# Sorting token-expert pairs by expert in a two-layer adaLN kernel: 46 gathered rows in place of all experts on all tokens

## The chip, the core and the metric

The kernel runs on one core of a Trainium2 chip. The core has five engines that work at the same time: TensorE (PE, matrix products into PSUM; PEld is its weight load), VectorE (DVE), ScalarE (ACT), GpSimd (POOL) and SyncE (SP, which issues DMAs). [...] DMAs issued on SP, ACT and POOL all run on the core's 16 DMA engines. The metric is the device time of one execution in microseconds (us), the median of several.

## What is computed

Two blocks of an adaLN network on x of 2 batches x 1024 tokens x 128 features, float32. The first block is a recurrence and six layers of windowed attention with a gated feed-forward part. The second is full attention (16 heads of 64, a bias by distance) and a mixture of experts. The change is in the last part only:

```python
E, F, TOP_K = 8, 512, 2
router_logits = xf @ gate_w                             # [2048, 8]
top_vals, top_idx = jax.lax.top_k(router_logits, TOP_K)
top_w = jax.nn.softmax(top_vals, axis=-1)
cw = jnp.einsum('tk,tke->te', top_w, one_hot(top_idx, E))   # 2 of 8 weights are not zero
for e in range(E):
    h = gelu(xf @ w1[e] + b1[e])                        # 128 -> 512
    out = out + cw[:, e:e + 1] * (h @ w2[e] + b2[e])    # 512 -> 128
```

Here xf is the layer-normed, scaled and shifted stream; the result is gated and added to the stream. Only two experts of each token have a weight other than zero.

## The kernel before

Tokens are worked on in four segments of 512 (two of each batch); features of a segment stand as [128 features, 512 tokens] or, turned, as four tiles of [128 tokens, 128 features]. All products are float32; each is two instructions on TensorE.

The first block (`first_block`, 0 to about 1635 us) writes out the order of PE, DVE, ACT and POOL by hand. The second (`second_block`) writes out PE, DVE and ACT; POOL and SP are placed by the tile scheduler. `attention` goes over 128 tiles of (batch, pair of heads, 128 query tokens), one every 5.86 us: turned probabilities of the tile two back, scores of this one, their maximum (DVE, line 1390), the exponential (ACT, line 1400), the scaling by the sum (POOL, line 1404), the output of the tile three back (line 1426). Once the last head of a segment is through, `attention_projected` (line 1436) makes the new stream and `expert_tokens` appends small pieces of work to a list: norm (`norm_pieces`: tokens, moments, centred, scaled), routing (`routing_pieces`: logits, exponentials, chosen, weights), expert biases (`bias_pieces`). `next_piece` runs one of them per tile, later one per expert. In `centred`, POOL makes `ln_less` (lines 1464, 1465) between two steps of ACT. Batch 0's pieces run in the attention of batch 1; part of batch 1's run in the expert stage.

The expert stage (`experts`) goes over 4 segments x 8 experts. `expert_hidden` makes the 512 hidden features of 512 tokens (line 1617: four products of 128x128 by 512; GELU on ACT, line 1620), `expert_outputs` the four tiles of output (line 1633: 16 products of 128x128 by 128) and adds each, times its token's weight for this expert, to `macc` (DVE, line 1637). `expert_sum` gates, adds the stream and writes the segment out. All weights of the eight experts stay in SBUF; two experts are loaded before the attention, six when it has ended (lines 1510, 1513). PSUM has four double banks throughout the second block.

Of the kernel before, what the change touches and what calls it, by code (L numbers as in the profile page):

```python
# [26 lines left out]
SEG = 512  # L28
# [24 lines left out]


# [37 lines left out]
class Net:  # L92
    def __init__(self, ctx, tc, io):
        self.ctx, self.tc, self.nc, self.io = ctx, tc, tc.nc, io
        nc = self.nc
        self.const = ctx.enter_context(tc.tile_pool(name="const", bufs=1))
        self.stream = ctx.enter_context(tc.tile_pool(name="stream", bufs=1))
        self.stat = ctx.enter_context(tc.tile_pool(name="stat", bufs=3))
        self.n = 0

        self.fixed = self.const.tile([128, NCONST], F32, tag="fixed", name="fixed")
        nc.scalar.dma_start(out=self.fixed[:, :K_TAB], in_=io["shape_consts"][:, :K_TAB])
        self.cols = self.const.tile([128, NCOLS], F32, tag="cols", name="cols")
        nc.scalar.dma_start(out=self.cols, in_=io["cols"])
        self.ident = self.fixed[:, K_ID : K_ID + 128]
        self.eps = self.const.tile([128, 1], F32, tag="eps", name="eps")
        nc.gpsimd.memset(self.eps, EPS)
# [95 lines left out]
    def recurrence_loads(self):  # L203
# [18 lines left out]
        nc.sync.dma_start(out=self.fixed[:, K_TAB:], in_=io["shape_consts"][:, K_TAB:])  # L222
# [693 lines left out]
    def rotary(self, st, a):  # L916
# [3 lines left out]
        if st.seg < PER_B:  # L920
# [4 lines left out]
            for kind in range(2):  # L925
                j = 2 * a + kind
                tab = self.fixed[:, K_TAB + j * NTT * DH : K_TAB + (j + 1) * NTT * DH]
                tab = tab.rearrange("p (t d) -> p t d", d=DH)[:, t0 : t0 + TT]
                for lo, width, other in ((0, DH, 0),) if kind == 0 else ((0, half, half), (half, half, 0)):
                    nc.gpsimd.tensor_tensor(  # L930
                        rot[:, kind, :, lo : lo + width],
                        tab[:, :, lo : lo + width],
                        sc[:, other : other + width].unsqueeze(1).to_broadcast([128, TT, width]),
                        ALU.mult,
                    )
# [276 lines left out]
    def second_block_opened(self):  # L1212
# [18 lines left out]
        for e in range(2):  # L1231
            self.load_expert(e)
# [10 lines left out]
    def second_block(self):  # L1243
# [4 lines left out]
        engines = {mybir.EngineType.PE, mybir.EngineType.DVE, mybir.EngineType.Activation}  # L1248
        with ExitStack() as es:
            self.psum(es, "two", 0, 4)  # L1250
            with ExitStack() as at:
                work = at.enter_context(tc.tile_pool(name="att_left", bufs=2, side="left"))
                with tc.manual_schedule(engines=engines):
                    self.attention(work)
            self.right.close()
            rest = es.enter_context(tc.tile_pool(name="moe_rest", bufs=2, side="left"))
            for e in range(2, E):
                self.load_expert(e, rest)
            with tc.manual_schedule(engines=engines):
                self.experts(rest)  # L1260
# [5 lines left out]
    def attention(self, work):  # L1266
# [10 lines left out]
        for n in range(len(tiles) + 3):  # L1277
# [19 lines left out]
            self.next_piece()  # L1297
            if last and lc == NP - 1 and lt % TT == TT - 1:
                seg = lb * PER_B + lt // TT
                self.attention_projected(seg, oT[lb])  # L1300
                self.expert_tokens(seg)
            if n < len(tiles) and t in (3, 5) and n + NKT - t < len(tiles):
# [140 lines left out]
    def norm_pieces(self, src, out, scale, bias, b, keep=None):  # L1443
# [15 lines left out]
        def centred():  # L1459
# [7 lines left out]
            for i in range(TT):  # L1467
# [6 lines left out]
                )  # L1474

# [31 lines left out]
    def load_expert(self, e, pool=None):  # L1507
        nc, io = self.nc, self.io
        w1 = self.get(pool or self.mw, [128, F1], f"ew1_{e}", bufs=1)
        nc.sync.dma_start(out=w1, in_=io["ew1"][e])  # L1510
        w2 = self.get(pool or self.mw, [128, F1 // 128, D], f"ew2_{e}", bufs=1)
        queue = nc.gpsimd if pool else nc.sync
        queue.dma_start(out=w2, in_=io["ew2"][e].rearrange("(c p) d -> p c d", p=128))
        self.ew[e] = w1, w2

    def expert_tokens(self, seg):

        b = seg // PER_B
        tokens = self.get(self.moe, [128, TT, D], "x_tok", bufs=NSEG)
        h = self.get(self.moe, [128, SEG], "mh", bufs=NSEG)  # L1520
        self.norm_pieces(self.x3, h, 4, 3, b, keep=tokens)
        cw = self.routing_pieces(h)
        acc = self.get(self.moe, [128, TT, D], "macc", bufs=NSEG)
        self.bias_pieces(cw, acc)
        self.routed[seg] = tokens, h, cw, acc

    def routing_pieces(self, h):
# [4 lines left out]
        cw = self.get(work, [128, TT, E], "cw", bufs=NSEG)  # L1532
        sel = self.get(work, [128, TT, E], "sel")
# [41 lines left out]
        return cw  # L1575
# [20 lines left out]
    def experts(self, work):  # L1596

        order = [(s, e) for s in range(NSEG) for e in range(E)]
        hidden = {}
        for n in range(len(order) + 1):  # L1600
            if n < len(order):
                hidden[n] = self.expert_hidden(work, *order[n])
            if n:
                self.expert_outputs(*order[n - 1], hidden.pop(n - 1))
            self.next_piece()
            if n and order[n - 1][1] == E - 1:
                self.expert_sum(work, order[n - 1][0])

    def expert_hidden(self, work, s, e):
        nc = self.nc  # L1610
        h, w1 = self.routed[s][1], self.ew[e][0]
        hid = self.get(work, [128, F1 // 128, SEG], "hid")
        for i in range(F1 // 256):
            ps = self.two_banks()
            for k in range(2):
                j = 2 * i + k
                nc.tensor.matmul(ps[:, k], w1[:, j * 128 : (j + 1) * 128], h, start=True, stop=True)  # L1617
            for k in range(2):
                j = 2 * i + k
                nc.scalar.activation(  # L1620
                    hid[:, j], ps[:, k], AF.Gelu, bias=self.col(C_EB1 + e * 4 + j)
                )
        return hid

    def expert_outputs(self, s, e, hid):
        nc = self.nc
        _, _, cw, acc = self.routed[s]
        w2 = self.ew[e][1]
        ps = self.bank()
        for t in range(TT):  # L1630
            tok = slice(t * 128, (t + 1) * 128)
            for j in range(F1 // 128):
                nc.tensor.matmul(  # L1633
                    ps[:, tok], hid[:, j, tok], w2[:, j], start=(j == 0), stop=(j == F1 // 128 - 1)
                )
        for t in range(TT):
            nc.vector.scalar_tensor_tensor(
                acc[:, t],
                ps[:, t * 128 : (t + 1) * 128],
                cw[:, t, e : e + 1],  # L1640
                acc[:, t],
                ALU.mult,
                ALU.add,
            )

    def expert_sum(self, work, s):
        nc = self.nc
        tokens, _, _, acc = self.routed[s]
        gate = self.gates[:, s // PER_B].unsqueeze(1).to_broadcast([128, TT, D])
        o = self.get(work, [128, TT, D], "o")  # L1650
        nc.vector.tensor_tensor(o, acc, gate, ALU.mult)
        nc.vector.tensor_tensor(o, o, tokens, ALU.add)
        nc.sync.dma_start(
            out=self.io["out"][s * SEG : (s + 1) * SEG].rearrange("(i p) d -> p i d", p=128), in_=o
        )
# [104 lines left out]
```

## Time and profile before

| | us |
|---|---|
| median of 3 runs (2808.8 to 2812.72) | 2810.84 |
| the profiled execution | 2810.53 |
| its span in the profile | 2808.8 |
| attention and all before it, to the last projection's end | 2572.4 |
| expert stage, to the end | 236.4 |
| busy in the span: PE / DVE / ACT / POOL | 2674.5 / 1917.5 / 1760.1 / 1582.8 |
| mean granted TensorE clock | 0.994 |
| all DMA: 37.62 MB, mean | 13 GB/s |

Times in the profile are counted from the span's start. A row of the timeline has the start, the duration, the engine, the source line, the operation, tiles as out<-in, the count, and in brackets the idle time before it with what ended that. The time of a page's line is busy time of that engine; engines overlap, so busy times do not add up to the span. "L1633" is line 1633 of the kernel before; the changed kernel has other line numbers.

### The profile page before, as it was taken

The numbers are of one execution on the slowest core, as the hardware profiler recorded it, in microseconds if no ns is written. First come the engines' busy times: TensorE is split into PE (matmuls) and PEld (weight loads), VectorE is DVE, ScalarE is ACT, GpSimd is POOL, SyncE is SP. The second block draws the span as 40 slices with busy tenths as digits, with TensorE's granted clock in tenths as the row PEclk, the third lists the DMA queues.
The fourth block names the chain that finished last, engine by engine and source line by source line (L and its number), as shares of the span: only waits on it lengthen the run. The fifth ranks groups of instructions, "written<-read, shape, count | busy, mean of one in ns | idle before, by whom it ended". The sixth has DMA issues, their size and how long they took to land.

```text
span 2808.8 us, 67320 instructions
## 1 busy us (share of the span) xinstructions
PE 2674.5 (95%) x29476; PEld 1784.6 (64%) x29476; DVE 1917.5 (68%) x2664; ACT 1760.1 (63%) x2514; POOL 1582.8 (56%) x1223
## 2 busy tenths in 40 slices
PE   7899999999999999999999989999999999999999
PEld 4466666666666666666666646666666666666776
DVE  6788788787878787888788746666566666663211
ACT  6467777777777677777777755555544555554533
POOL 4687888788787878788788613333333333331000
PEclk9999999999999999999999999999999999999999
DMA  3000100000010001000000010000000000001000
GB/s 132 1 2 2 32 2 9 32 2 2 9 32 2 6 4 32 2 9 2 2 2 2 17 53 7 10 10 7 7 11 7 7 7 7 1 1 46 4 5 8
DMA packets 24208, 37.62 MB, mean 13 GB/s; under 512 B 1862, under 2 KB 19404, under 8 KB 22892
## 3 DMA queue, kind: packets, MB, share of 16 engines
q1 hardware_dynamic: 22780, 30.29, 3.5%
q8 instruction: 232, 3.80, 0.6%
q0 software_dynamic: 704, 2.43, 0.3%
q10 hardware_dynamic: 432, 0.61, 0.1%
q14 instruction: 60, 0.49, 0.1%
HBM read 32.24 MB, written 1.08 MB: 12 GB/s over the span
## 4 chain that ended last, share of the span: by engine, by line
PE 68%; ACT 15%; DVE 12%; issue 3%; POOL 2%; DMA 0%; ACTq 0%; POOLq 0%; DVEq 0%
PE two L1374 8%; PE proj L948 8%; PE two L1413 7%; PE two L1426 6%; PE two L1123 5%; PE two L1104 5%; ACT px L1113 4%; PE two L1633 4%; PE two L1617 4%; PE two L1019 4%; DVE turned L974 2%; PE two L1039 2%; DVE qk L967 2%; PE two L1190 2%; PE two L1204 2%
## 5 line engine op out<-in xcount | busy, mean ns | idle before, releaser
L1404 POOL TENSOR_SCALAR ap<-ap,a_den 128x1024 f32<-128x1024 f32 x256 | 283.9, 1121 | 578.3 <-DVE a_den L1403 578.2
L985 POOL TENSOR_TENSOR qk<-qk,turned 128x1024 f32<-128x1024 f32 x192 | 453.8, 2363 | 192.1 <-DVE turned L974 185.2
L1400 ACT ACTIVATE ap<-two,a_neg 128x1024 f32<-128x1024 f32 x256 | 285.1, 1114 | 294.2 <-DVE a_neg L1390 287.8
L1390 DVE TENSOR_REDUCE a_neg<-two 128x1 f32<-128x1024 f32 x256 | 301.1, 1217 | 170.7 <-PE two L1374 170.7
L1123 PEld LDWEIGHTS two<-px,wvo 128*128 128x128 f32 x3072 | 356.7, 192 | 57.2 <-issue 29.9
L948 PE MATMUL proj<-wqk,xs 128*128 128x512 f32 x764 | 370.6, 608 | 22.6 <-DVE turned L974 21.1
L1123 PE MATMUL two<-px,wvo 128*128 128x128 f32 x3072 | 362.0, 276 | 17.3 <-ACT xw L1085 17.1
L997 POOL TENSOR_TENSOR qk<-qk,w_inv 128x1024 f32<-128x1024 f32 x192 | 361.7, 1906 | 3.9 <-ACT w_inv L994 2.9
L1413 PEld LDWEIGHTS two<-fixed,ap 128*128 128x128 f32 x2048 | 223.4, 141 | 138.6 <-issue 122.0
L1413 PE MATMUL two<-fixed,ap 128*128 128x128 f32 x2048 | 277.6, 279 | 15.0 <-ACT ap L1400 12.6
L959 ACT ACTIVATE sq<-proj 128x1024 f32<-128x1024 f32 x191 | 195.9, 1026 | 134.3 <-PE proj L948 133.5
L967 DVE TENSOR_TENSOR qk<-proj,rot 128x1024 f32<-128x1024 f32 x191 | 232.5, 1217 | 49.4 <-ACT sq L959 43.9
L1374 PE MATMUL two<-ak,aq 64*128 64x512 f32 x1024 | 259.3, 618 | 2.9 <-DVE gates L1505 1.6
L1426 PE MATMUL two<-apT,av 128*64 128x128 f32 x4096 | 254.2, 277 | 4.3 <-ACT apT L1416 4.3
L1113 ACT COPY px<-two 128x1024 f32<-128x1024 f32 x192 | 195.1, 1017 | 76.5 <-PE two L1104 76.5
L1426 PEld LDWEIGHTS two<-apT,av 128*64 128x64 f32 x4096 | 223.2, 138 | 25.4 <-issue 20.5
L1071 POOL TENSOR_TENSOR p<-p,w_den 128x1024 f32<-128x1024 f32 x96 | 183.3, 1909 | 98.1 <-DVE ya L1133 86.3
L1019 PEld LDWEIGHTS two<-fixed,qk 128*128 128x128 f32 x1536 | 165.1, 141 | 110.9 <-issue 80.9
L974 DVE TENSOR_TENSOR turned<-proj,rot 128x1024 f32<-128x1024 f32 x191 | 231.8, 1213 | 1.5 <-POOL qk L985 1.5
L948 PEld LDWEIGHTS proj<-wqk,xs 128*128 128x128 f32 x764 | 133.1, 191 | 147.2 <-issue 110.9
L1019 PE MATMUL two<-fixed,qk 128*128 128x128 f32 x1536 | 204.1, 277 | 20.7 <-ACT px L1113 13.0
L982 DVE TENSOR_REDUCE w_ss<-sq 128x16 f32<-128x1024 f32 x192 | 221.2, 1191 | 1.5 <-ACT sq L959 1.5
(271 smaller groups left out, 4310.9 us busy)
## 6 DMA issues: line engine op xcount, KB each, us to landing
wqk<-in_wqkv SPq DMA_DIRECT2D x6, 1024.0 KB, 11.5
abias<-rel_turned SPq DMA_DIRECT2D x32, 192.0 KB, 3.0
wv<-in_wqkv SPq DMA_DIRECT2D x6, 512.0 KB, 3.6
wo<-in_wo SPq DMA_DIRECT2D x6, 512.0 KB, 4.1
ew<-in_ew SPq DMA_DIRECT2D x10, 256.0 KB, 4.1
w<-in_w SPq DMA_DIRECT2D x6, 341.0 KB, 8.4
aqkv<-in_aqkv SPq DMA_DIRECT2D x1, 1536.0 KB, 6.7
ew<-in_ew POOLq DMA_DIRECT2D x6, 256.0 KB, 6.8
```

Of the source, the lines that this page charges most:

```text
L948: self.nc.tensor.matmul(ps[:, g], x.step.xs[:, c0 : c0 + 128], x.step.weights[:, a, g * 512 : (g + 1) * 512], start=True, stop=True,)
L967: nc.vector.tensor_tensor(dst, ps.rearrange("p a (h d) -> p (a h) d", d=DH), cos.unsqueeze(1).to_broadcast([128, H, DH]), ALU.mult,)
L974: nc.vector.tensor_tensor(x.turned, halves[:, :, ::-1], sin.rearrange("p (e d) -> p e d", e=2).unsqueeze(1).to_broadcast([128, H, 2, half] ...
L985: self.nc.gpsimd.tensor_tensor(x.qk[a], x.qk[a], x.turned.rearrange("p h e d -> p h (e d)"), ALU.add)
L997: engine.tensor_tensor(x.qk[a], x.qk[a], x.inv[:, a].unsqueeze(2).to_broadcast([128, H, DH]), ALU.mult)
L1019: nc.tensor.transpose(ps[:, c // 4, c % 4 * 128 : (c % 4 + 1) * 128], flat[:, c * 128 : (c + 1) * 128], self.ident,)
L1113: self.nc.scalar.copy(x.px[:, 2 * i : 2 * i + 2].rearrange("p b h q -> p b (h q)"), x.mixed[i])
L1123: nc.tensor.matmul(x.out[:, 0, :128].rearrange("p (b q) -> p b q", q=BLK), merged[:, c // 4, par, c % 4], x.px[:, :, h], start=(h == 0), s ...
L1374: nc.tensor.matmul(scores[par][:, j], q[r, tok], k[r, j * 512 : (j + 1) * 512], start=True, stop=True)
L1390: self.nc.vector.tensor_reduce(neg, ps, AX.XY, ALU.max, negate=True)
L1413: self.nc.tensor.transpose(ps[:, j // 4, j % 4 * 128 : (j % 4 + 1) * 128], p[:, j * 128 : (j + 1) * 128], self.ident)
L1426: nc.tensor.matmul(ops[r, :128], v[:, j, r], pT[par][:, j], start=(j == 0), stop=(j == NKT - 1))
```

## The change

A batch has 1024 tokens and so 2048 pairs of token and chosen expert. The pairs are sorted by expert into rows of 128 slots, each expert beginning a new row: 23 rows (`ROWS = 2 * NKT + E - 1`) hold any choice; what isn't filled is padding. A row has one expert.

Once both segments of a batch are routed, five new pieces (`dispatch_pieces`) make the plan: `counted` (TensorE: how many pairs of an expert stand before each token, and the totals), `placed` (DVE: each pair's slot and each row's expert), `spread` (DVE: one-hot tiles of slot places and token numbers), `listed` (TensorE: their products are the token number of each slot) and `shared` (DVE: the two weights of each token). `centred` also writes the centred tokens to memory. Each row then is gathered from there by an indirect DMA on POOL, turned by TensorE, scaled and shifted, sent through its expert, and written to memory; each token's two outputs are gathered back from there and summed. The weights of a row's expert are loaded for each row anew, from a table in memory (4112 B for each of 128 partitions) that is built beforehand; SP reads the expert's number into a register first. PSUM is eight single banks in the expert stage. In this stage the order of POOL and SP is written out by hand, too.

In `experts`, step n turns row n, makes the hidden features of row n - 1 and the outputs of row n - 3, and runs two pieces. Batch 1's 23 gathers are issued when its plan is there; the condition `(1, 0) not in gathered` holds again in the step after row (1, 0) was taken, and the 23 are issued a second time. POOL's order is: 10 gathers of batch 0 in the attention (with the weights of two rows on SP); 13 at the start of the stage; the last segment's `ln_less`; 23 and 23 of batch 1; 16 of token outputs of batch 0; 16 of batch 1. The token sums of batch 0 begin at step 29, one tile every two steps.

```diff
         with ExitStack() as es:
-            self.psum(es, "two", 0, 4)
+            self.disp = es.enter_context(tc.tile_pool(name="dispatch", bufs=1, side="left"))
+            self.dispatch_tables()
             with ExitStack() as at:
+                self.psum(at, "two", 0, 4)
                 with tc.manual_schedule(engines=engines):
                     self.attention(work)
             self.right.close()
-            for e in range(2, E):
-                self.load_expert(e, rest)
-            with tc.manual_schedule(engines=engines):
+            self.psum(es, "moe", 8, 0)
+            with tc.manual_schedule(engines=engines | {ET.Pool, ET.SP}):
                 self.experts(rest)
...
             self.next_piece()
+            if n >= len(tiles):
+                self.next_piece()
...
                 self.expert_tokens(seg)
+                if seg % PER_B == PER_B - 1:
+                    self.dispatch_pieces(lb)
...
+            if home is not None:
+                nc.sync.dma_start(out=home, in_=xc)
...
+    def dispatch_tables(self):
+        self.table = home("expert_rows", [E, 128, EW])
+        nc.sync.dma_start(out=self.table[:, :, :F1], in_=io["ew1"])
+        for e in range(E):
+            nc.sync.dma_start(
+                out=self.table[e, :, F1 : 2 * F1].rearrange("p (c d) -> p c d", d=D),
+                in_=io["ew2"][e].rearrange("(c p) d -> p c d", p=128),
+            )
...
+    def dispatch_pieces(self, b):
+        def counted():
+            nc.tensor.matmul(ps[:, : NKT * E], self.earlier, flat, start=True, stop=False)
...
+        def spread():
+            for c in range(2):
+                hot = self.onehot().rearrange("p (t f) -> p t f", f=128)
+                nc.vector.tensor_tensor(
+                    hot,
+                    place[:, c * NKT : (c + 1) * NKT].unsqueeze(2).to_broadcast([128, NKT, 128]),
+                    self.count.unsqueeze(1).to_broadcast([128, NKT, 128]),
+                    ALU.is_equal,
+                )
...
+        def listed():
+            for i, (c, t) in enumerate(pairs):
+                nc.tensor.matmul(ps[:, :ROWS], st["hot"][c][:, t], st["ids"][:, c, t], start=i == 0, stop=i == len(pairs) - 1)
...
+        self.pieces += [counted, placed, spread, listed, shared]
...
     def experts(self, work):
-        order = [(s, e) for s in range(NSEG) for e in range(E)]
+        order = [(b, j) for b in range(B) for j in range(ROWS)]
+        for j in range(len(gathered), ROWS):
+            gathered[0, j] = self.slots_gathered(work, 0, j)
+        for n in range(len(order) + 4):
             if n < len(order):
-                hidden[n] = self.expert_hidden(work, *order[n])
+                while loads < len(order) and loads < n + 12 and order[loads][0] in self.plan:
+                    weights[loads] = self.row_weights(work, *order[loads])
+                    loads += 1
+            if n < len(order):
+                if order[n][0] == 1 and (1, 0) not in gathered:
+                    for j in range(ROWS):
+                        gathered[1, j] = self.slots_gathered(work, 1, j)
+                feats[n] = self.row_features(work, order[n][0], gathered.pop(order[n]))
+            if 0 <= n - 1 < len(order):
+                hidden[n - 1] = self.row_hidden(work, feats.pop(n - 1), weights[n - 1])
+            if 0 <= n - 3 < len(order):
+                self.row_outputs(work, *order[n - 3], hidden.pop(n - 3), weights.pop(n - 3))
+            for _ in range(2):
+                self.next_piece()
+            k = n - ROWS
+            if n >= ROWS + 6 and (k - 6) % 2 == 0 and (k - 6) // 2 < NKT:
+                self.token_sums(work, 0, (k - 6) // 2)
+            if 1 in self.plan and (1, 0) not in gathered and n < ROWS - 1:
+                for j in range(ROWS):
+                    gathered[1, j] = self.slots_gathered(work, 1, j)
+        for t in range(NKT):
+            self.token_sums(work, 1, t)
...
+    def slots_gathered(self, work, b, j, bufs=ROWS):
+        x = self.get(work, [128, D], "slots", bufs=bufs)
+        self.nc.gpsimd.indirect_dma_start(
+            x, None, self.centred_rows[b], bass.IndirectOffsetOnAxis(self.plan[b][1][:, j : j + 1], axis=0)
+        )
+    def row_weights(self, work, b, j, bufs=12):
+        e = nc.values_load(self.plan[b][0][0:1, j : j + 1], engines={mybir.EngineType.SP}, min_val=0, max_val=E - 1)
+        w = self.get(work, [128, EW], "row_w", bufs=bufs)
+        nc.sync.dma_start(out=w, in_=self.table[bass.ds(e, 1)].rearrange("o p c -> (o p) c"))
+    def row_features(self, work, b, x):
+        nc.tensor.transpose(ps[:, :128], x, self.ident)
+        nc.vector.tensor_scalar(
+            h, ps[:, :128], self.mod1[:, 4, b : b + 1], self.mod1[:, 3, b : b + 1], ALU.mult, ALU.add
+        )
+    def row_hidden(self, work, h, w):
...
+    def row_outputs(self, work, b, j, hid, w):
...
+        y = self.get(work, [128, D], "row_y", bufs=4)
+        nc.vector.tensor_copy(y, ps[:, :D])
+        nc.sync.dma_start(out=self.output_rows[b][j * 128 : (j + 1) * 128], in_=y)
+    def token_sums(self, work, b, t):
+        for c in range(2):
+            y = self.get(work, [128, D], "pair_y", bufs=2 * NKT)
+            nc.gpsimd.indirect_dma_start(
+                y, None, self.output_rows[b], bass.IndirectOffsetOnAxis(slots[:, c, t : t + 1], axis=0)
+            )
+            nc.vector.scalar_tensor_tensor(
+                acc[:, i], y, share[:, c, t : t + 1], acc[:, i], ALU.mult, ALU.add
+            )
+        nc.vector.tensor_tensor(o, acc[:, i], self.gates[:, b], ALU.mult)
+        nc.vector.tensor_tensor(o, o, tokens[:, i], ALU.add)
+        nc.sync.dma_start(out=self.io["out"][seg * SEG + i * 128 : seg * SEG + (i + 1) * 128], in_=o)
```

## The prediction

> **What bounds the kernel now.** I read the page's busy shares first, then the chain of waits from the end of the attention on, then the stretch tables for the DMA rate, then the timeline for the price of one POOL transfer and for the slack of the engines around it.
>
> The page (engine totals; the shares of the chain):
>
> ```profile
> PE 2674.5 (95%) x29476; PEld 1784.6 (64%) x29476; DVE 1917.5 (68%) x2664; ACT 1760.1 (63%) x2514; POOL 1582.8 (56%) x1223
> ...
> PE 68%; ACT 15%; DVE 12%; issue 3%; POOL 2%; DMA 0%; ACTq 0%; POOLq 0%; DVEq 0%
> ```
>
> TensorE is the bound, and DMA is nowhere. The chain of waits in the expert stage (start, duration, engine, tile, line, instructions):
>
> ```profile
> 2583.89 3.44 PE two L1617 x8
> 2587.33 3.57 PE two L1633 x32
> 2590.90 3.44 PE two L1617 x8
> ```
>
> One expert on one segment of 512 tokens is 7.01 us of TensorE with nothing between, and there are 32 of them. The stretch table (busy us of PE, PEld, DVE, ACT, POOL; granted clock; DMA share; GB/s):
>
> ```profile
> 2572.40:2808.80 236.40, 230.46 (x1329) 168.39 (x1327) 50.16 (x171) 95.87 (x149) 4.97 (x8) 1.00 0.06 19
> ...
> 2575.00:2577.00 2.00, 2.00 (x12) 1.44 (x11) 0.18 (x1) 1.55 (x4) 2.00 (x4) 1.00 1.03 363
> 2577.00:2579.00 2.00, 2.00 (x6) 0.89 (x5) 0.01 (x1) 0.65 (x2) 0.44 (x1) 1.00 1.03 341
> 2579.00:2581.00 2.00, 2.00 (x12) 1.28 (x11) 0.00 (x0) 1.55 (x4) 0.00 (x0) 1.00 1.05 331
> ```
>
> The stage to be replaced lasts 236.4 us at full clock; with all DMA engines busy (share 1) the core reads 331 to 363 GB/s. The timeline, first the price of a POOL transfer, then the slack of POOL in the attention, then the end:
>
> ```profile
> 1.30 1.30 POOL L171 DMA_DIRECT2D sq<-in_wmod  x2 [0.46 <-issue]
> ...
> 2500.93 2.21 POOL L1404 TENSOR_SCALAR ap<-ap,a_den 128x1024 f32<-128x1024 f32 x2 [4.20 <-DVE a_den L1403]
> ...
> 2505.85 1.09 PE L1413 MATMUL two<-fixed,ap 128*128 128x128 f32 x8
> 2506.68 2.21 POOL L1404 TENSOR_SCALAR ap<-ap,a_den 128x1024 f32<-128x1024 f32 x2 [3.54 <-DVE a_den L1403]
> ...
> 2572.86 4.58 POOL L1513 DMA_DIRECT2D ew<-in_ew  x6 [10.17 <-PE two L1436]
> ...
> 2805.50 0.37 SPq L1653 DMA_DIRECT2D out<-o  x1
> ```
>
> POOL issues a plain transfer of 128 rows in 0.65 us (1.30 for two) and one of 512 pieces in 0.76. In the attention it has 3.65 us free in each 5.86 us tile, and a scaled tile (first half done at 2502.0) is wanted 3.8 us later.
>
> **What TensorE saves.** A row of 128 slots is one transpose (0.11 us) and 8 products of 128x128, two instructions each: 16 x 0.112 (3.57 / 32) = 1.8; together 1.9 us. 46 rows are 87 us, against 32 x 7.01 = 224 us. The 896 slots of padding in 2944 are in that. The saving of 137 us is the most there is; the rest says what takes the place of TensorE.
>
> **The unknown price: one gather on POOL, g.** The trace has no indirect transfer. Below, the nearest row is the plain transfer of 128 rows, 0.65 us; above, the longest single POOL instruction of the running kernel, 2.36 us (line 985, two inputs of 128x1024). A gather also has 128 indices to read and 128 addresses to make, so I take twice the plain row, 1.3 us: nearer to the lower end, which is the same kind of instruction. POOL's order in the changed kernel has 101 gathers: 10 in the attention, 13 at the start of the stage, 23 for batch 1, the same 23 again (the condition in `experts` is true a second time once row (1,0) is taken), 16 pairs for batch 0, 16 for batch 1.
> [...]
>
> **The attention of batch 1, where batch 0 is sorted.** TensorE is full there, so its new work is paid: counting and listing are 16 products each, 64 instructions of 0.12 us (0.95 for 8 at line 1538), 7.6 us. DVE has 1.6 us free per tile (5.86 less 2.35, 1.21, 0.45, 0.27). Placing is 13 small operations, 2.8 us (0.18 for 32 elements a row, 0.41 for 256); spreading is 5.0 (two of 128x1024 at 1.21, the others 0.2 to 0.55). Over by 1.2 and 3.4; the rings of scores and turned tiles hide between all and none of that, I take 2.5 lost. The 10 gathers stand on POOL ahead of the next scaling: 13 less 3.65 free less 3.8 slack, 5.6 us for TensorE. Sum **+15.7**. At nothing: building the table in memory (10 copies on SP in layer 0, around layer 1's last two loads, which go out at 31 us and are due over 200 us later; uncovered, 4.2 MB in and out at 345 GB/s would be an estimated 25 us); the writes of centred rows (256 KB, landing 2.3 us by the out rows; batch 0's have 25 tiles before they are read, batch 1's last stands behind twelve weight loads, 12 x 1.5 = 18 us, and is read after t = 47; if late, the same microseconds on every later step); the rotary tables, which only move to another pool; the dropped expert loads, which were hidden. On SP the two first rows' register and weight loads (1 MB, 3.1 us) stand ahead of bias loads that have a lead of some five tiles, 29 us.
>
> **The stage, from 2572.4 on (t = 0: the last projection ends).**
> 1. POOL's 13 gathers wait for the attention's buffers, and the last segment's `ln_less` (lines 1464, 1465 before) is now queued behind them. ScalarE stands at it in order, with it the GELUs of the rows, and TensorE at the next transpose. 13 x 1.3 + 0.5 (ln_less) + 1.65 (centring) + 0.2 + 0.66 + 0.78 + 1.1 (transposes, features, logits) = **21.8**. Some three rows run meanwhile.
> 2. Five steps with two pieces each: exponentials with two table loads of 1.28 and four GELUs of 0.41, 4.4; weights, 2.3; biases and counting on TensorE, 1.9 + 1.1 + 3.8 = 6.8; placing and spreading on DVE, 7.9, then listing, 3.8, and a copy: 12. Tokens of batch 1 are there at **47.3**.
> 3. From here the pace of a row. TensorE 1.9. DMA: 526 KB of weights, 66 KB out, 66 KB gathered, at 331 to 363 GB/s: 1.8 to 2.0. The output buffers: row r's write stands on SP behind the load that waits for row r+2, and its buffer is due again at r+4, so load issue 0.43, write issue 0.43, the load's 1.5 and a landing of 2.3 (the out rows' median) go into two rows: 2.3 each. ScalarE 1.65. I take 2.3; reading the register on SP has no row and is taken as hidden.
> 4. POOL runs 46 gathers from 47.3: 107.1, then the first pair, 109.7, landed 112.0. DVE wants it at step 29, 47.3 + 20 x 2.3 = 93.3, and stands with the rows' features behind it. TensorE resumes at step 31 at 112.5, and 17.5 steps later, 152.8, the last row is done.
> 5. The tail: copy, write, landing 3.0; 16 gathers 20.8 and a landing 2.3; sums 0.9; output 3.3 (2805.5 to 2808.8). End at **183.1**.
> Against 236.4 the stage wins 53.3. The profiled execution took 2810.5 (span 2808.8), 0.3 under the median of 2810.8: 2810.5 - 53.3 + 15.7 = **2773 us**.
>
> **The ends for g.** At 0.65: step 1 is 13.3, tokens at 38.8, POOL never late, last row at 130, end at 150, attention +10: 2734. At 2.36: step 1 35.6, tokens at 61, first pair at 177, last row at 217, end at 264, attention +26: 2865. Between, 1 us of g is worth 87 us, and g = 1.73 breaks even.
>
> **The rivals.**
> A, slower: a gather costs over 1.73 us. Place: POOL between t = 47 and the first pair, and the tail. For it: nothing on POOL that reads a value per row is in the trace, and its element work is slow (2.36 for 128x1024 against 1.21 on DVE). Against: 512 pieces cost only 0.1 more than 128, so rows are cheap there. Time at the upper end 2865.
> B, gathers as cheap as plain transfers: rows paced by DMA and the output buffers alone, 2734.
> C, SP or the weight stream sets the pace: register load, a load and a write for each row in one queue. At 3.5 us a row the first 20 steps lose 24, of which the 18.7 of waiting at step 29 absorb most, and the last 17.5 lose 21: +26, 2800. For it: no register load is in the trace; against: SP issues in 0.33 to 0.43, and the loads run twelve rows ahead.
> That the change doesn't do what it says is partly so already: the double gathers are in the sum; without them POOL would be 30 us earlier and the wait at step 29 gone.
>
> **How the numbers follow.** Forecast 0.46; B 0.16; C 0.10 (0.08 still faster, 0.02 slower); A 0.24; no change that can be told (within 0.2%, about what a measurement of this kernel can tell) 0.04, the crossing between forecast and A. Faster 0.70, slower 0.26. The range leaves out the cheapest fifth of B and the dearest third of A: 2735 to 2850; the forecast's own, for g from 0.95 to 1.6, is 2742 to 2800.
>
> **What would show it.** Right: 101 indirect transfers on POOL of about 1.3 us; ScalarE idle for some 12 us behind `ln_less` just after the last projection; DVE idle before the first `pair_y` sum; a tail of 25 to 30 us in which only POOL works; TensorE under half busy in the last 180 us. Wrong: gathers over 1.7 us; rows at 3 us or more that wait for `row_w`; an attention that has grown by more than 25 us.

## The result: 1.2% slower, where a gain was forecast

The changed kernel takes 2844.35 us (median of 4 runs, 2843.08 to 2845.33) beside 2811.59 for the kernel before on the same chip: a ratio of 1.0118, with a 95% interval of 1.0100 to 1.0135. The profiled execution has a span of 2842.4 us against 2808.8. The last projection now ends some 30.5 us later, at about 2602.9, and the expert stage behind it lasts 239.5 us instead of 236.4. The forecast had 15.7 and 183.1. In the stage TensorE's busy time fell from 230.5 to 130.0 us, and yet the stage became 3 us longer.

The page of the kernel after (busy us, share of the span, instructions), and the rows of its 40 slices for TensorE, POOL and the granted clock:

```profile
PE 2598.3 (91%) x29106; PEld 1755.4 (62%) x29106; DVE 1944.4 (68%) x2741; ACT 1728.6 (61%) x2568; POOL 1675.6 (59%) x1322
...
PE   8799999999999999999999989999999999997664
...
POOL 3587888788788878887888523333332343332342
PEclk9899999999999999999999999999999999998687
```

TensorE has 76 us less to do and is still the busiest engine, but in the last four slices, 71 us each, it is no longer full, and its clock is no longer either. The stretch table of the kernel after (busy us and instructions of PE, PEld, DVE, ACT, POOL; clock; DMA share; GB/s) for the whole stage, for a piece of it in which TensorE stood, and for a piece in which it ran:

```profile
2602.90:2842.40 239.50, 130.03 (x887) 122.79 (x886) 63.07 (x210) 65.78 (x203) 87.20 (x93) 0.74 0.47 140
...
2680.70:2696.90 16.20, 0.06 (x1) 0.00 (x0) 0.70 (x2) 1.14 (x4) 10.72 (x13) 0.63 0.35 78
2728.00:2735.00 7.00, 6.08 (x53) 5.87 (x54) 1.22 (x4) 4.26 (x16) 3.77 (x5) 1.00 0.95 324
```

TensorE, where it was full before, is busy for little more than half of the stage. No other engine is the bound: none is busy for more than POOL's 87 of 239 us, and the DMA engines work at less than half. In the 16.2 us of the middle row POOL is nearly the only engine at work (ScalarE has 1.14 us in it, DVE 0.70). The timeline of the kernel after around that row shows why that is odd:

```profile
2676.59 1.06 PE L1885 MATMUL bank<-row_w,row_hid 128*128 128x128 f32 x8
...
2677.48 0.27 PE L1857 MATMUL bank<-fixed,slots 128*128 128x128 f32 x1
...
2679.60 1.06 PE L1885 MATMUL bank<-row_w,row_hid 128*128 128x128 f32 x8
...
2683.20 1.14 ACT L1873 ACTIVATE row_hid<-bank,row_w 128x128 f32<-128x128 f32 x4 [7.16 <-issue]
...
2693.63 0.95 POOL L1835 DMA_INDIRECT slots<-centred,tokens  x1 [0.30 <-issue]
2693.68 0.33 SPq L1851 DMA_DIRECT2D row_w<-expert_rows  x1
2693.69 0.29 DVE L1893 COPY row_y<-bank 128x128 f32<-128x128 f32 x1 [15.14 <-remote]
...
2696.48 0.41 DVE L1859 TENSOR_SCALAR row_h<-bank,mod 128x128 f32<-128x128 f32 x1 [2.50 <-remote]
...
2696.95 2.08 PE L1869 MATMUL bank<-row_h,row_w 128*128 128x128 f32 x8 [16.18 <-issue]
```

The products of row 8's outputs stand at 2676.59 and end, as modelled, at 2677.65. DVE needs nothing but them for its copy (line 1893), and yet goes on at 2693.69, 16 us later; SP's next weight load waits for the same products and goes in the same moment. The transpose of row 12, at 2677.48, reaches DVE (line 1859) at 2696.48. TensorE, which needs that copy for the next products, stands for 16.18 us. The profile calls the releaser "remote": it finds no instruction that ended then. From 2669.7 on POOL had been issuing one gather (line 1835) after the other, 0.95 us each with 0.30 between. The same picture stands beside every burst of gathers: ScalarE and DVE wait for a "remote" until 2622.43 and 2622.46 behind the burst of 13, and until 2313.6 behind the ten in the attention. So the theory that I tested, called H in the expectations, is: while POOL issues indirect transfers one behind the other, TensorE's results come to the other engines late. Whether the products themselves are late or only the word of them, these rows do not tell, since the ends of products are modelled. The expectations set H against P, the view of the prediction (a gather costs POOL's time alone), and W (rows wait for their weights or for output buffers).

### The profile page after: what moved, and what is told of

Its sections match the earlier page's. It is cut to its first block, busy times and chain, and to the rows that moved or that the text cites. A ratio compares the mean times of both kernels' runs of the same rounds, so it can differ in the third digit from the quotient of the medians.

```text
span 2842.4 us, 67310 instructions
## 1 busy us (share of the span) xinstructions
PE 2598.3 (91%) x29106; PEld 1755.4 (62%) x29106; DVE 1944.4 (68%) x2741; ACT 1728.6 (61%) x2568; POOL 1675.6 (59%) x1322
## 5 line engine op out<-in xcount | busy, mean ns | idle before, releaser
L1129 PEld LDWEIGHTS two<-px,wvo 128*128 128x128 f32 x3072 | 357.4, 193 | 56.4 <-issue 29.0
```

The costliest lines, as they stand in the source:

```text
L1129: nc.tensor.matmul(x.out[:, 0, :128].rearrange("p (b q) -> p b q", q=BLK), merged[:, c // 4, par, c % 4], x.px[:, :, h], start=(h == 0), s ...
```

## The experiments

**A gather by itself, beside the kernel before.** The kernel before has an idle POOL in the expert stage. Into its ninth step go 40 transfers whose data nothing reads:

```diff
+            if n == 8:
+                self.side_rows(work)
...
+        for i in range(40):
+            x = self.get(work, [128, D], "side", bufs=8)
+            nc.gpsimd.indirect_dma_start(
+                x, None, self.io["x"], bass.IndirectOffsetOnAxis(ids[:, 0:1], axis=0)
+            )
```

> The kernel before the change with 40 gathers of 128 rows of 512 bytes issued by POOL in the expert stage, beside the experts; nothing reads what they bring, the output is the same. Theory H: for 40 x 1.255 = 50 us TensorE's results come late, and the stage, which needs three of them for each 7 us expert, is 10 to 45 us longer: 2821 to 2856. Theories P and W: POOL was idle there and nothing waits for it, so 2809 to 2814.

The control has a plain transfer of the same size on the same queue:

```diff
-            nc.gpsimd.indirect_dma_start(
-                x, None, self.io["x"], bass.IndirectOffsetOnAxis(ids[:, 0:1], axis=0)
-            )
+            nc.gpsimd.dma_start(out=x, in_=self.io["x"][:128])
```

> The same as the kernel with 40 side gathers, but with 40 plain transfers of 128 rows of 512 bytes on POOL in place of the indirect ones. Theory H with the indirect form as the cause: no change, 2809 to 2814. Theory H with any POOL transfer as the cause: as long as with the gathers, or in proportion to POOL's time (26 us of transfers), 5 to 25 us more. P and W: no change.

Measured: 2849.77 us with the gathers, ratio 1.0146 (1.0122 to 1.0169), 39.2 us over the kernel before; 2810.79 with the plain transfers, ratio 1.0005 (0.9993 to 1.0017). Forty gathers that nobody waits for cost 39 us; forty plain transfers nothing. The waits of the kernel with side gathers between 2636 and 2688 us, while POOL issues (engine, line, waited for, us, times, longest), and its timeline:

```profile
PE two L1652 <- issue: 29.0, 7, 16.5
DVE macc L1656 <- remote: 25.9, 1, 25.9
```

```profile
2668.16 1.12 DVE L1656 SCALAR_TENSOR_TENSOR macc<-two,cw,macc 128x128 f32<-128x128 f32 x4 [25.90 <-remote]
2669.34 4.00 PE L1652 MATMUL two<-ew,hid 128*128 128x128 f32 x17 [16.48 <-issue]
2674.46 0.37 PE L1652 MATMUL two<-ew,hid 128*128 128x128 f32 x1 [1.13 <-issue]
2676.57 0.37 PE L1652 MATMUL two<-ew,hid 128*128 128x128 f32 x1 [1.74 <-issue]
2677.96 0.28 PEld L1652 LDWEIGHTS two<-ew,hid 128*128 128x128 f32 x1 [1.81 <-issue]
2679.36 0.37 PE L1652 MATMUL two<-ew,hid 128*128 128x128 f32 x1 [2.42 <-issue]
2680.76 0.29 PEld L1652 LDWEIGHTS two<-ew,hid 128*128 128x128 f32 x1 [2.52 <-issue]
2682.16 0.37 PE L1652 MATMUL two<-ew,hid 128*128 128x128 f32 x1 [2.42 <-issue]
2684.96 0.37 PE L1652 MATMUL two<-ew,hid 128*128 128x128 f32 x1 [2.43 <-issue]
```

First the same "remote" releaser. From 2674 on TensorE itself is slow: one product instruction and one weight load in each 2.80 us, where the trace of before has 32 such pairs in 3.57. They belong to a group of products that had begun at 2669.34, and the profile shows nothing that they wait for. So it is not only the word of finished products that is late, and "results come late" is a short name for what is seen; how the two hang together is open.

**What it goes with.** Two variants: gathers of 16 rows instead of 128, and gathers of 128 rows with some other work of POOL between.

```diff
-                x, None, self.io["x"], bass.IndirectOffsetOnAxis(ids[:, 0:1], axis=0)
+                x[:16], None, self.io["x"], bass.IndirectOffsetOnAxis(ids[:16, 0:1], axis=0)
```

> The kernel before the change with 40 side gathers back to back, each of 16 rows of 512 bytes instead of 128. If the loss goes with the rows or bytes, or with POOL's time and that falls: under 10 us over the kernel before. If it goes with the instruction, whatever its size: 35 to 45 us over it, as with 128 rows.

```diff
                 x, None, self.io["x"], bass.IndirectOffsetOnAxis(ids[:, 0:1], axis=0)
             )
+            rest = self.get(work, [128, 512], "rest", bufs=2)
+            nc.gpsimd.tensor_tensor(rest, self.fixed[:, :512], self.fixed[:, :512], ALU.add)
```

> The kernel before the change with 40 side gathers as in the earlier run, but with an addition of 128x512 on POOL behind each, an estimated 1.2 us by half of the 2.36 for two inputs of 128x1024, so one gather every 2.5 us. Theory H, with results passing in the pauses: 0 to 10 us over the kernel before, 2811 to 2821. Rival B (a fixed loss for each gather): 35 to 45 us over it, as when they stood back to back.

Measured: 2851.40 with 16 rows, ratio 1.0147 (1.0129 to 1.0166), the same loss as with 128; 2809.87 with additions between, ratio 1.0009 (0.9996 to 1.0021), no loss. The loss goes neither with rows nor with bytes nor with the number of gathers, but with their standing back to back. Nor are the DMA engines full: in the stretch with the 16-row gathers their share is 0.04 (the last number but one; TensorE is busy for 22.03 of 54 us):

```profile
2636.00:2690.00 54.00, 22.03 (x96) 13.79 (x94) 2.09 (x6) 8.09 (x13) 34.72 (x41) 0.65 0.04 11
```

The timeline of POOL in the kernel with spaced side gathers:

```profile
2638.45 0.98 POOL L1624 DMA_INDIRECT side<-in_x,ids  x1 [0.16 <-issue]
2639.45 1.05 POOL L1628 TENSOR_TENSOR rest<-fixed 128x512 f32<-128x512 f32 x1
2640.65 0.97 POOL L1624 DMA_INDIRECT side<-in_x,ids  x1 [0.16 <-issue]
2641.64 1.05 POOL L1628 TENSOR_TENSOR rest<-fixed 128x512 f32<-128x512 f32 x1
```

Here one gather every 2.2 us was harmless, one every 1.26 (128 rows) or 1.16 (16 rows) was not. The fixed loss for each gather, called rival B in the expectations, is out.

**In the changed kernel: fewer gathers, and other transfers.** First the doubled 23 gathers are taken out:

```diff
-                if order[n][0] == 1 and (1, 0) not in gathered:
+                if order[n] == (1, 0) and (1, 0) not in gathered:
```

> The changed kernel with the rows of batch 1 gathered once instead of twice: 78 gathers on POOL instead of 101, the same output. Theory H (while POOL runs indirect transfers, TensorE's finished products are reported to the other engines late): between 2707 and 2738 us the second set of 23 gathers, 28.9 us at 1.255 each, no longer holds up rows, and 15 to 25 us go, to some 2820 to 2830. Theory P, mine of the prediction (a gather costs POOL's time alone): POOL stood idle for 17.95 us before the first pair, waiting for outputs, so 23 gathers less on it bring nothing: 2841 to 2847. Theory W (rows wait for their weights or for output buffers): nothing either.

> The changed kernel with each of its 101 gathers replaced by a plain transfer of 128 rows of 512 bytes on the same queue (the rows read are the last 128 of the buffer, so the dispatch is not computed; pairs wait only for the last row's write). Theory H with the indirect form as the cause: the holding up ends, the four bursts lose some 10 us each and POOL's time falls from 1.255 to 0.65 a transfer: 2760 to 2800. Theory H with any POOL transfer as the cause: only POOL's time falls, 8 us at the start and 10 in the tail: 2820 to 2830. Theories P and W: the same 2820 to 2830.

```diff
-        self.nc.gpsimd.indirect_dma_start(
-            x, None, self.centred_rows[b], bass.IndirectOffsetOnAxis(self.plan[b][1][:, j : j + 1], axis=0)
-        )
+        if j == 0 or (b, j) == (0, 10):
+            gate = self.get(self.disp, [128, 1], "gate", bufs=2)
+            self.nc.gpsimd.tensor_copy(gate, self.plan[b][1][:, j : j + 1])
+        self.nc.gpsimd.dma_start(out=x, in_=self.centred_rows[b][N - 128 :])
...
-            nc.gpsimd.indirect_dma_start(
-                y, None, self.output_rows[b], bass.IndirectOffsetOnAxis(slots[:, c, t : t + 1], axis=0)
-            )
+            nc.gpsimd.dma_start(out=y, in_=self.output_rows[b][(ROWS - 1) * 128 :])
```

The kernel with plain transfers leaves out what the sorting found: it moves the same 128 rows each time. The small copy (`gate`) makes its bursts begin when the gathers did.

Measured: 2815.44 with the rows gathered once, ratio 1.0021 (1.0011 to 1.0031): 28 to 29 us gone, about as much as 23 gathers take at 1.255 us and 3 to 4 us more than the 15 to 25 that H expected, though POOL had stood idle for 17.95 us before the first pair. With plain transfers 2774.29, ratio 0.9869 (0.9845 to 0.9894), 70 us below the changed kernel; within theory H's range with the indirect form as the cause, and 46 us under the least that a saving of POOL's time alone was expected to give.

**More work on POOL, nothing else.** The sharpest test between H and my own theory of a price in POOL's time (P): an addition behind every gather of the stage but the last 16, in the changed kernel and in the one that gathers once.

```diff
+        if work is not self.disp:
+            self.pause(work)
...
+            if b == 0:
+                self.pause(work)
...
+    def pause(self, work):
+        rest = self.get(work, [128, 256], "rest", bufs=2)
+        self.nc.gpsimd.tensor_tensor(rest, self.fixed[:, :256], self.fixed[:, :256], ALU.add)
```

> The changed kernel with one thing added and nothing taken away: behind each gather of the stage, the last 16 and the ten in the attention excepted, POOL does an addition of 128x256 that nothing reads (some 0.6 us). POOL has 45 us more to do. Theory H: the bursts no longer hold TensorE's results up, and although the 46 gathers of batch 1 now last to some 2755, the kernel gets faster, 2815 to 2830. Theory P (POOL's time is what gathers cost): work added to POOL can only lengthen it, 2850 to 2875.

> The kernel that gathers once, 2815, with the same addition behind each gather of the stage but the last 16; nothing else is moved. Theory H: the 15 rows that stood in the bursts of 23 and 16 come at 1.9 to 2.3 us a row, 20 to 35 us go: 2780 to 2795. Theory P: 2815 to 2840.

Measured: 2832.78, ratio 1.0075 (1.0058 to 1.0093), and 2798.16, ratio 0.9959 (0.9940 to 0.9979). Useless work on POOL makes the one kernel 10 to 12 us faster (by the ratios and by the medians) and the other 17; the intervals are apart from those without it. Both are 3 us outside H's range, on the side of a smaller gain, and far from P's.

In the stage of the second no "remote" stands among the waits that come to 20 us or more; in the changed kernel DVE's copies of row outputs alone waited for one for 42.9 us. Why the gain is no larger can be read from the trace of the first, with 101 gathers. The price that P names is there too: the gathers follow one another more slowly, and some of them come late themselves. TensorE waits 12.70 us for a gathered row and stands 25.82 us at a step where DVE, in its order, waits for the first pair:

```profile
2718.68 0.48 PE L1863 MATMUL bank<-fixed,slots 128*128 128x128 f32 x1 [12.70 <-DMA slots<-centred,tokens]
...
2757.50 0.35 DVE L1915 SCALAR_TENSOR_TENSOR macc<-pair_y,share,macc 128x128 f32<-128x128 f32 x1 [22.87 <-DMA pair_y<-outputs,slots]
...
2761.06 2.05 PE L1875 MATMUL bank<-row_h,row_w 128*128 128x128 f32 x8 [25.82 <-issue]
```

**Pacing them by waits.** Here a row's gather stands behind the transpose four rows earlier, and has to wait for its buffer; the pairs have four buffers.

```diff
                 feats[n] = self.row_features(work, order[n][0], gathered.pop(order[n]))
+                if n + 4 < len(order) and order[n + 4] not in gathered:
+                    gathered[order[n + 4]] = self.slots_gathered(work, *order[n + 4], 4)
...
-            y = self.get(work, [128, D], "pair_y", bufs=2 * NKT)
+            y = self.get(work, [128, D], "pair_y", bufs=4)
```

> The changed kernel with 78 gathers, and in the stage each row's gather put right behind the transpose four rows earlier (four slot buffers instead of 23), each pair's behind the sum two tokens' tiles earlier (four buffers instead of 16); same output. Theory H, with results passing in the pause between spaced gathers: the hold-ups of the bursts of 13, 23 and 16 go, some 30 to 60 us against the 2815 of the kernel that gathers once: 2750 to 2785. Rival B (each gather costs TensorE the same wherever it stands): 2800 to 2820. Rival L (rows now wait for their gather to land): over 2820.

> As the paced kernel, and besides the ten gathers in the attention stand one by one between POOL's scalings, and row weights are loaded up to eight rows ahead instead of twelve, so that no load waits for a buffer and no write of a row stands behind such a load. Theory H: the burst of ten cost some 7 us, the writes' wait some us more: 5 to 15 us below the paced kernel. Rival B: the ten cost the same one by one, and loads were early anyway: within 4 us of the paced kernel.

```diff
-                while loads < len(order) and loads < n + 12 and order[loads][0] in self.plan:
+                while loads < len(order) and loads < n + 8 and order[loads][0] in self.plan:
...
-                self.first_rows(10, 2)
+                for j in range(10):
+                    self.pieces.append(lambda j=j: self.first_row(j))
+                self.pieces.append(lambda: self.first_rows(0, 2))
```

Measured: 2801.74, ratio 0.9967 (0.9953 to 0.9982), and 2791.60, ratio 0.9932 (0.9912 to 0.9951). Both are faster than the kernel before. But the first number lies at the edge of rival B's range, not in H's; the second is in H's. The stretch table of the paced kernel with more shows what I had missed:

```profile
2660.00:2697.00 37.00, 36.52 (x328) 36.33 (x327) 11.94 (x39) 21.93 (x77) 18.55 (x20) 1.00 0.99 323
2697.00:2761.00 64.00, 44.95 (x301) 43.70 (x300) 20.30 (x67) 19.45 (x68) 26.04 (x28) 0.79 0.51 148
```

With one gather in 1.9 us TensorE is full and a row takes 1.9 us. From 2697 on, rows and pairs share POOL, three or four gathers stand together again, and TensorE stands four times for 3.0 to 5.5 us (2704.11, idle 5.46); 18 rows take 64 us. These stands can't be put down to H alone: in the 64 us DVE waits 16.0 us for pairs that POOL has only just begun to gather (4.82 us until 2701.80) and 0.7 us for a "remote", and the rows' features stand behind the pairs in its order. The additional edit is worth 10 us. Some 6 of them are won in the attention: in the changed kernel the burst of ten cost 6.7 us of delay (the same score products, 19.1 late at 2308, 25.8 late at 2321), and here, where the ten stand one by one, 0.7 us.

**All gathers spaced by POOL itself.** The additions behind the gathers again, the rows of a batch handed to POOL two a step, pairs of batch 0 four steps later, the rest as in the paced kernel with more; once with one piece of the sorting behind each row, once with two.

```diff
+        todo = [(0, j) for j in range(len(gathered), ROWS)]
...
-            for _ in range(2):
-                self.next_piece()
+            self.next_piece()
...
-            if n >= ROWS + 6 and (k - 6) % 2 == 0 and (k - 6) // 2 < NKT:
+            if n >= ROWS + 10 and (k - 10) % 2 == 0 and (k - 10) // 2 < NKT:
...
+            if 1 in self.plan and loads1:
+                todo += [(1, j) for j in range(ROWS)]
+                loads1 = False
+            for row in todo[:2]:
+                gathered[row] = self.slots_gathered(work, *row)
+            todo = todo[2:]
```

> As the paced kernel with more, but the gathers of the stage are spaced by POOL itself: behind each stands an addition of 128x256, an estimated 0.6 us, which nothing reads, so one gather every 1.9 us; slot and pair buffers are 23 and 16 again, pairs of batch 0 begin four steps later, and one piece of the sorting stands behind each row instead of two. Theory H (only back-to-back gathers hold TensorE's results up): the 18 rows beside batch 0's pairs, 64 us in the run before, come down to some 35 to 45, and the pieces hide better: 2750 to 2775. Rival S (those rows are slow for another reason, DVE's sums or the output writes): 2783 to 2797.

> The same with two pieces of the sorting behind each row, as in the changed kernel. If the pieces' chain of waits, and not the gathers, sets the first 58 us of the stage, this is 5 to 15 us slower than with one piece; if gathers set it, the two are within 3 us.

Measured: 2768.74, ratio 0.9853 (0.9824 to 0.9882), and 2776.13, ratio 0.9875 (0.9849 to 0.9902). The first is the best kernel here, 41 us under the kernel before; with the computation that the change asked for and 78 gathers in it. Whether one piece is better than two stays unclear, since the intervals overlap. The stretch table of the spaced kernel for its stage and for 26 us out of it, and the timeline:

```profile
2600.70:2768.80 168.10, 111.59 (x887) 107.08 (x886) 66.39 (x210) 65.80 (x203) 98.97 (x122) 0.85 0.59 191
2670.00:2696.00 26.00, 26.00 (x236) 26.00 (x235) 8.09 (x27) 15.61 (x56) 23.37 (x30) 1.00 1.04 381
```

```profile
2673.05 0.97 POOL L1844 DMA_INDIRECT slots<-centred,tokens  x1 [0.16 <-issue]
...
2673.45 0.27 PE L1868 MATMUL bank<-fixed,slots 128*128 128x128 f32 x1
2673.56 1.06 PE L1880 MATMUL bank<-row_h,row_w 128*128 128x128 f32 x8
...
2674.04 0.62 POOL L1832 TENSOR_TENSOR rest<-fixed 128x256 f32<-128x256 f32 x1
...
2674.46 1.06 PE L1896 MATMUL bank<-row_w,row_hid 128*128 128x128 f32 x8
...
2674.82 0.97 POOL L1844 DMA_INDIRECT slots<-centred,tokens  x1 [0.16 <-issue]
...
2703.92 0.35 DVE L1920 SCALAR_TENSOR_TENSOR macc<-pair_y,share,macc 128x128 f32<-128x128 f32 x1 [9.12 <-DMA pair_y<-outputs,slots]
...
2707.48 2.05 PE L1880 MATMUL bank<-row_h,row_w 128*128 128x128 f32 x8 [11.00 <-issue]
```

In the 26 us POOL issues a gather every 1.77 us, and TensorE, at full clock, is busy without a gap. The last two lines are the longest stand that is left, and it is again of P's kind: DVE waits for the first pair, which POOL takes up behind the last row. So a good part of what this kernel wins over the paced ones may be the order of pairs and rows and the larger pair buffers; what the spacing alone is worth was measured in the two kernels with additions above.

## Why the prediction was wrong, by its own steps

**What TensorE saves: right.** A row was put at 1.9 us and takes 1.90 wherever nothing holds it up.

**The price of a gather, g: right in size, wrong in kind.** It was put at 1.3 us and is 1.255 (0.95 busy, 0.30 idle), under the 1.73 at which the kernel would break even. The side gather of 16 rows took 0.85 us against 0.95 for 128, so by an estimate from these two a row costs about 1 ns. The step that failed is the one that turned g into time: "1 us of g is worth 87 us" counted a gather as POOL's time alone, and asked only who waits for POOL. (By the prediction's own ends it is 87 us above g = 1.3, and 60 below.) The kernel with 40 side gathers shows a cost of one microsecond each to TensorE (39.2 us in all) with nobody waiting. Rival A has the right sign, but its mechanism, g over 1.73, did not happen. The forecast's rival B, cheap gathers, can be read off the kernel with plain transfers (0.55 us each): 2774.3 where B had 2734, with a stage of some 167 us (B: 150) and an attention some 31 us longer (B: 10).

**The attention, +15.7: it was 30.5.** By the starts of the same score products in the two traces: some 3 us were there before the sorting began (put at nothing; in the traces of other variants this part is 0.9 to 8.5 us, so it is in part chance), 15.2 came with counting, placing, spreading and listing (put at 10.1), 6.7 with the ten gathers (put at 5.6, for another reason: POOL's next scaling, not TensorE's results), and 4.8 with the third segment's routing, whose transposes and logits now stand before the last projection (not seen). The sorting was under-sized most in one tile, from 2286 to 2300, where the delay grows by 7.8 us: TensorE stands 2.31 us there while DVE spreads, and listing takes 5.05 us, not 3.8. The rest, 1.1 us, came in the tile behind the listing, from 2300 to 2308. The ten gathers were taken apart by two runs, one by one in the paced kernel with more and as plain transfers: 0.7 us each time. The other parts no run took one by one.

**Step 1, the stall at the last segment's `ln_less`, 21.8: the logits end at t = 31.1.** The wait is there, but not where I put it. The gathers ended at 2620.1, and `ln_less` began at 2626.78, after waiting 6.66 us for ScalarE, which had stood until 2622.43 at a GELU (the row with "remote" in the kernel after):

```profile
2622.43 1.14 ACT L1873 ACTIVATE row_hid<-bank,row_w 128x128 f32<-128x128 f32 x4 [7.89 <-remote]
...
2626.78 0.20 POOL L1481 TENSOR_TENSOR ln_less<-ln_mv,ln_rstd 128x4 f32<-128x4 f32 x1 [6.66 <-ACT ln_rstd L1479]
```

**Step 2, tokens of batch 1 at 47.3: at 66.5.** Of the 19.2 us, 9.3 are step 1's. Listing took 6.99 us, not 3.8: TensorE, after its idle stretches, was granted half its clock (0.50 from 2662.0 to 2669.3). That was nowhere in the sum, since the trace of before had 1.00 in the stage.

**Step 3, 2.3 us a row: 3.8 on the mean of the 37 rows from 2669.0 to 2810.4.** This is the largest error, and H, with the clock that was lost behind long stands (0.50 behind the one of 16.18 us), is its cause: rows beside gathers that are spaced take 1.9 to 2.3 on the mean (1.90 in the spaced kernel's 26 us, 2.3 beside its pairs). Rival C, the weight stream, was wrong: by the DMA packets in the trace the weights of row 14 had landed at 2642.8 and were used at 2709.3, and SP's register loads took 0.27 us at the median. Taking the load-ahead down from twelve rows to eight did no harm.

**Step 4, the first pair landed at 112 because POOL is late: POOL was not late.** It stood for 17.95 us waiting for row outputs and issued the first pair at t = 153. The rows, not the gathers ahead of it, set its time.

**Step 5, the tail of 30.3 us: 32.1.** Right. Here TensorE has nothing to do, and back-to-back gathers harm nobody.

So the sum erred by 14.8 us in the attention and by 56.4 in the stage. With the hold-up taken away by plain transfers or by spacing, the stage comes to some 167 and 168 us, under the 183.1 of the forecast; but these two kernels differ from the forecast's in more than that (transfers of 0.55 us in the one; 23 gathers fewer and another order in the other).

## What to carry to other kernels

Before work goes to an engine that "has time", ask what its instructions do to the others while they run, and if no row of a trace shows it, run forty of them beside the old kernel with a control of another kind: two kernels settle what a sum cannot. In these runs forty gathers issued back to back by POOL (one every 1.26 us) beside TensorE work that others waited for cost 39.2 us, so such bursts should not stand there; one every 1.8 to 2.2 us, paced by a buffer or by some other work on POOL, held up TensorE in no row looked at here. The time on POOL still counts: whoever waits for a gather waits longer behind paced ones (12.70 and 25.82 us in the kernel with 101 of them). When all engines idle together and the profile names no releaser, look for the engine that is the only one at work.

## What the runs showed of the hardware that I had not expected

- Back-to-back indirect transfers on POOL (one every 1.16 to 1.26 us) held up TensorE's results: in the rows shown, 16 to 20 us for one result (with side gathers ScalarE waited 47.2 us for a "remote": the GELU of a product that ended, as modelled, at 2652.86 began at 2693.44, 40 us later), then one product instruction and one weight load of TensorE every 2.80 us. 0.30 us between two gathers were too little; 0.95 us of idling (in the paced kernel with more, until 2697), or an addition of 0.62 us (in the spaced kernel) or 1.05 us (in the kernel with spaced side gathers), were enough. Plain transfers of POOL, 0.54 us each back to back, did nothing of the kind (ratio 1.0005). DVE's results did not come late in the same stretch: with side gathers its sums end at 2669.28, and TensorE goes on at 2669.34. Why it is so, and why the first five to nine gathers of a burst did little harm, is open; no run here looked into it.
- The clock was lower after such stands: after the 16.18 us at 2696.95 the granted clock was 0.50 until 2700.7, and eight TensorE instructions took 2.08 us; from 2709.2 on, at 1.00, they took 1.06. In the whole stage 887 TensorE instructions were busy for 130.0 us at a mean clock of 0.74 in the changed kernel, and for 111.6 at 0.85 in the spaced one. A much shorter stand, of 2.69 us before 2313.90 by a modelled end, was followed by a clock of 0.50 too, from 2313.9 to 2318. How long a stand has to be for this no run here shows.
- A gather cost POOL almost the same for 16 rows as for 128: 0.85 and 0.95 us.
